# A recurrent block times a mixture of experts: four successive tokens per partition

## The chip, the core and the metric

The kernel runs on one core of a Trainium2 chip. The core has a matrix engine (TensorE, in the profile PE, with its weight loads as PEld), a vector engine (VectorE, DVE), an activation engine (ScalarE, ACT), GpSimd (POOL) and SyncE (SP), which here issues transfers only. Each engine runs its own queue in order and waits on semaphores for the others. On-chip memory is SBUF, and PSUM takes the results of matmuls; both have 128 partitions. [...]

The metric is device time in microseconds (us) from start to end of one execution. Lower is better.

## What is computed

The input `x` is (16, 512, 256) in fp32: 16 sequences, 512 tokens, 256 channels. The reference, cut to what matters:

```python
x  = L0_attn_x
xn = layernorm(x)
s  = rwkv(xn)                 # along time in each sequence
g  = silu(moe(xn))            # 8 experts; tokens are given out by top-k
return x + s * g

# rwkv(x)
x  = ln(x, ln0_w, ln0_b); h = ln(x, ln1_w, ln1_b)
xx = time_shift(h)                         # the token before
xk = h*tmk + xx*(1 - tmk)                  # and xv, xr likewise
k, v, sr = xk @ Wk.T, xv @ Wv.T, sigmoid(xr @ Wr.T)
att  = scan over t of a running weighted mean of v, weights exp(k)
x  = x + (sr*att) @ Wo.T
h2 = ln(x, ln2_w, ln2_b)
xk2, xr2 = mixes of h2 and its time shift
kv = square(relu(xk2 @ Wfk.T)) @ Wfv.T
return x + sigmoid(xr2 @ Wfr.T) * kv

# moe(x): xt is (8192, 256)
probs = softmax(xt @ Wg)
for each expert: its 1024 best tokens      # ties by token number
each token goes to its best expert among those that took it
out = weight * (gelu(xt @ W1[e]) @ W2[e])
```

Two orders matter. Time shift, the scan and the breaking of ties need a sequence's tokens in time order. A matmul that gives tokens on partitions can take them in any order, as long as everything else uses the same.

## The kernel before, in words

A sequence `b` has 512 tokens. In token-major tiles (`x`, `n`, `x0`, `y`, `s`) it is a tile of 128 partitions by `NJ` = 4 by 256 channels. `rows_of` (line 169) maps DRAM to it with `(j p) c -> p j c`: block `j` of 128 successive tokens, one token of each block on a partition. A partition thus holds tokens 128 apart, and each DMA piece is one row of 256 fp32, 1 KB. In channel-major tiles (`hp`, `mix_*`, `kT`, `vT`, `erT`, `kf`) channels lie on partitions and the 512 tokens in the free dimension.

**Start.** `logits(b)` (line 232) loads a sequence as `xa`, normalizes it to `xn`, stores that to `xn_d`, transposes it on TensorE (line 219), copies the transpose out of PSUM (line 245, on ACT or DVE) and adds the router's logits to `lg`. `route` (line 256) follows: transposes, softmax, a search bit by bit for each expert's threshold, and scans (lines 345, 408) that need time order. Its pieces are issued after projections of the recurrence (`then_route`). At the end it builds by matmul (lines 431 to 463) a table of which token each slot of an expert holds: `holds` and `goes`. `row` (partition) and `tile_no` (block) give the token's number there.

**Recurrence.** `recurrent(b)` (line 578) is a generator of 9 steps. `normed` normalizes; `shifted` (line 483) transposes the result and evicts it with weight and bias into `hp`, one column to the right, so that `hp[:, h, 0:T]` is the shifted one (line 488). `mix` makes `a*h + (1-a)*shifted` with one ACT multiplication (line 495) and one DVE instruction (line 496). `project` (line 525) multiplies by a weight, 128 output channels by 512 tokens. `wkv` (line 535) runs the scans and ends with line 567, which writes the result over `v`. `token_major` (line 569) takes 128 tokens of a channel-major tile as the stationary operand and gives token-major output; it serves `Wo`, `Wfr` and `Wfv`. The hidden layer `kf` is evicted with Relu (line 632) and squared (line 633). `L627` copies `x` to `out` from DRAM to DRAM.

**Experts.** `expert(i)` (line 655) loads `W1` and `W2` of its expert, gathers 2 x 128 rows of `xn_d` by index (line 664), and scatters its results to `ys_d` by index (line 695).

**Outputs.** For `b` below 14 `keep` (line 731) stores the recurrence's result in `s_d`; `outputs` loads it again as `s` with `y` from `ys_d`, applies Silu (line 727), multiplies (line 728) and adds to `out` by an accumulating DMA issued by POOL (line 729). The last two sequences go there directly (`put`).

The order is written by hand: `steps` (lines 759 to 764) interleaves three sequences, and `rest_of` deals out the logits of sequences 4 to 15 over steps 0 to 5, the 36 sure expert units over steps 24 to 124, the outputs from step 124 on. Buffers: `x`, `w1`, `w2` two each, `tok` three, `f4` four, three PSUM banks for projections (`mm`).

Of the kernel before, what the change touches and what calls it, by code (L numbers as in the profile page):

```python
# [9 lines left out]
F32 = mybir.dt.float32  # L10
I32 = mybir.dt.int32
BF16 = mybir.dt.bfloat16
AF = mybir.ActivationFunctionType
ALU = mybir.AluOpType
# [5 lines left out]
P = 128  # L20
# [6 lines left out]
def rwkv_times_moe_kernel(ctx: ExitStack, tc: tile.TileContext, a, out: bass.AP):  # L27
# [67 lines left out]
    nc.vector.tensor_copy(count, up)  # L95
    count_s = const.tile([P, P], BF16, name="count_s")
    nc.vector.tensor_copy(count_s, up)
# [7 lines left out]

    tiles = iota("tiles", [[1, NJ], [NJ, B]] + [[0, P // NT]])
    tile_no = const.tile([P, NT], F32, name="tile_no")
    nc.vector.tensor_copy(tile_no, tiles.rearrange("p (t r) -> p t r", r=P // NT)[:, :, 0])
    ones = const.tile([P, 1], F32, name="ones")
# [59 lines left out]
    def rows_of(t, b):  # L169
        return t[b * T : (b + 1) * T].rearrange("(j p) c -> p j c", p=P)  # L170

    x_rows, out_rows = x.rearrange("b t c -> (b t) c"), out.rearrange("b t c -> (b t) c")


# [12 lines left out]
    def load(src, b, name, tag="x", bufs=2):  # L187
        t = work.tile([P, NJ, C], F32, tag=tag, bufs=bufs, name=f"{name}{b}")
        nc.sync.dma_start(t, rows_of(src, b))
        return t  # L190
# [24 lines left out]
    def transposed(src, h, name):  # L215

        ps = pp_tr.tile([P, T], F32, tag="tr", name=f"{name}_{h}")
        for j in range(NJ):
            nc.tensor.transpose(ps[:, j * P : (j + 1) * P], src[:, j, h * P : (h + 1) * P], ident)
        return ps  # L220
# [11 lines left out]
    def logits(b):  # L232
        g = slice(b * NJ, (b + 1) * NJ)
        xt = load(x_rows, b, "xa", tag=("w1", "w2")[b % 2])
        mv, rs = mv_all[:, g, :], rs_all[:, g]
        moments(mv, xt, f"a{b}")
        inv_std(rs, mv[:, :, 1])
        xn = work.tile([P, NJ, C], F32, tag="kf", bufs=KF, name=f"xn{b}")
        normalize(xn, xt, mv[:, :, 0], rs, f"a{b}")
        nc.sync.dma_start(rows_of(xn_d, b), xn)  # L240
# [15 lines left out]
    def route():  # L256
# [4 lines left out]
        ]  # L261
        nc.vector.tensor_copy(buf[0], lg)
        yield
# [89 lines left out]
        for j in range(NJ):  # L353
            nc.tensor.transpose(ps2[:, j * P : (j + 1) * P], gt[:, j * P : (j + 1) * P], ident)
        nc.vector.tensor_copy(buf[2], ps2)
# [68 lines left out]
        nc.vector.tensor_single_scalar(lo_i, slot, P - 1, ALU.bitwise_and)  # L424
        lo = work.tile([P, NT], BF16, tag="lo", name="lo")
# [57 lines left out]
    def shifted(n, wname, bname, name):  # L483

        hp = in_turn(hps)
        for h in range(NC):
            ps = transposed(n, h, f"nps_{name}")
            nc.scalar.activation(hp[:, h, 1:], ps, AF.Identity, bias=col(bname, h), scale=col(wname, h))
        return hp

    def mix(hp, tm, name):

        m = f4(f"mix_{name}")
        for h in range(NC):
            nc.scalar.mul(m[:, h, :], hp[:, h, 0:T], col(tm, h, rest))
            nc.vector.scalar_tensor_tensor(  # L496
                m[:, h, :], hp[:, h, 1:], col(tm, h), m[:, h, :], ALU.mult, ALU.add
            )
        return m
# [25 lines left out]
    def project(w, src, o, name):  # L525

        ps = pp_mm.tile([P, T], F32, tag="mm", name=name)
        for h in range(NC):
            mm = nc.tensor.matmul(  # L529
                ps, lhsT=w[:, h, o * P : (o + 1) * P], rhs=src[:, h, :], start=(h == 0), stop=(h == NC - 1)  # L530
            )
        then_route(mm)
        return ps

    def wkv(kT, vT, erT, h, name):
# [30 lines left out]
        nc.vector.reciprocal(den, den)  # L566
        nc.vector.tensor_tensor(v, ba0[:, 1, :], den, ALU.mult)

# [9 lines left out]
    def recurrent(b, done):  # L578
# [46 lines left out]
        xk2 = mix(hp2, "cmk", f"k2{b}")  # L625
        xr2 = mix(hp2, "cmr", f"r2{b}")
        nc.sync.dma_start(rows_of(out_rows, b), rows_of(x_rows, b))  # L627
        kf = []
        for q in range(NH // 2):
            t = work.tile([P, 2, T], F32, tag="kf", bufs=KF, name=f"kf{b}_{q}")  # L630
            for o in range(2):
                nc.scalar.activation(t[:, o, :], project(wfk, xk2, q * 2 + o, f"f_{b}_{q}_{o}"), AF.Relu)  # L632
            nc.scalar.activation(t, t, AF.Square)  # L633
            kf.append(t)
# [89 lines left out]
    def output(b, s, y):  # L724
        for j in range(NJ):
            t = j * B + b
            nc.scalar.activation(y[:, j, :], y[:, j, :], AF.Silu, scale=weight_of[:, t : t + 1])  # L727
        nc.vector.tensor_tensor(s, s, y, ALU.mult)
# [101 lines left out]
```

## Time and profile before

| | |
|---|---|
| median of 3 runs | 1306.62 us (1304.05 to 1310.38) |
| the profiled execution | 1304.01 us, its span 1302.2 us |
| mean granted TensorE clock | 0.941 |
| weight loads for TensorE | 778.3 us, 60% of the span |
| ACT, DVE busy | 733.3 us (56%), 762.6 us (59%) |
| DMA from SP's queue | 88,044 packets, 97.02 MB, 23.3% of 16 engines' span |
| DMA from POOL's queue | 15,360 packets, 27.27 MB, 9.4% |
| out store (line 729), issue to landing | 5.8 to 8.5 us |

The profile is one execution recorded by the hardware. An engine's busy time is the sum over its instructions. A group of instructions is shown as line, engine, operation, what it writes and reads, shapes and count; after the bar come busy time in all, the mean of one in ns, and how long the engine was idle just before them with what ended the wait. In a timeline a row is start, duration, engine, line, operation, and in brackets the idle time before it. Span rows by stage give each engine's busy time with the number of its instructions, then the clock granted to TensorE, the mean busy share of the 16 DMA engines and GB/s. The forty slices show the busy share in tenths.

### The profile page before, as it was taken

Reading aid. Unit: us, or ns where it says so; the run is one execution under the profiler, and the core shown is the slowest. Engines: PE = TensorE matmul, PEld = TensorE weight load, DVE = VectorE, ACT = ScalarE, POOL = GpSimd, SP = SyncE. Lnnn points to the kernel's source line nnn. Section 1 sums busy time; section 2 is a strip of 40 time slices with the busy share of each in tenths; the row PEclk is TensorE's granted clock in tenths of the full one; section 3 lists DMA queues with packets and bytes.
Section 4 is the critical chain, followed back from the end, with each engine's and each line's share of the span. In section 5 each row is a group of like instructions: output and inputs, shape, how many; then the busy total and the mean of one; then the engine's idle time right before and its main releaser. Section 6 shows DMA issues by size and latency. Waiting matters only on the chain. (4 is left out here: it accounts for less than half of the span.)

```text
span 1302.2 us, 12606 instructions
## 1 busy us (share of the span) xinstructions
PE 1141.6 (88%) x4333; PEld 778.3 (60%) x4333; DVE 762.6 (59%) x1248; ACT 733.3 (56%) x1187; POOL 333.3 (26%) x427
## 2 busy tenths in 40 slices
PE   5687979569989999899989999898999989795966
PEld 2344645335848667585856768585766857463635
DVE  4699675995481745647273565717456363566651
ACT  3685766137373655738275572728448283684951
POOL 3442030042312324132151423214231230213020
PEclk7799999788989999999999999999999999898978
DMA  6895010211303313131221423122322310278391
GB/s 200 289 297 151 1 33 1 81 41 33 109 12 114 101 61 130 49 125 52 85 94 50 129 79 97 51 84 94 95 83 68 110 66 17 98 158 206 84 191 24
DMA packets 103469, 125.11 MB, mean 96 GB/s; under 512 B 5847, under 2 KB 89325, under 8 KB 103405
## 3 DMA queue, kind: packets, MB, share of 16 engines
q1 hardware_dynamic: 88044, 97.02, 23.3%
q0 software_dynamic: 15360, 27.27, 9.4%
q8 instruction: 35, 0.57, 0.2%
q14 instruction: 30, 0.24, 0.1%
HBM read 90.72 MB, written 41.94 MB: 102 GB/s over the span
## 5 line engine op out<-in xcount | busy, mean ns | idle before, releaser
L529 PE MATMUL f<-mix_k,WfkT_sb 128*128 128x512 f32 x512 | 241.0, 627 | 28.2 <-DVE mix_k L496 23.2
L572 PE MATMUL kv<-WfvT_sb,kf 128*128 128x256 f32 x1024 | 228.9, 380 | 0.0
L695 POOL DMA_INDIRECT ys_d<-ys,goes x72 | 75.9, 1054 | 528.5 <-ACT ys L693 333.4
L572 PEld LDWEIGHTS kv<-WfvT_sb,kf 128*128 128x128 f32 x1024 | 193.6, 190 | 25.9
L529 PEld LDWEIGHTS f<-mix_k,WfkT_sb 128*128 128x128 f32 x512 | 100.0, 201 | 153.1 <-issue 105.2
L646 DVE SCALAR_TENSOR_TENSOR frs<-frs,kv 128x512 f32<-128x512 f32 x32 | 21.9, 683 | 249.0 <-PE kv L572 249.0
L572 PE MATMUL y<-w,act 128*128 128x256 f32 x576 | 132.1, 379 | 0.2 <-ACT act L686 0.2
L681 PE MATMUL h<-xsT,w 128*128 128x256 f32 x576 | 130.2, 379 | 0.0
L572 PEld LDWEIGHTS y<-w,act 128*128 128x128 f32 x576 | 107.7, 190 | 19.9 <-issue 5.9
L681 PEld LDWEIGHTS h<-xsT,w 128*128 128x128 f32 x576 | 109.4, 190 | 16.2 <-issue 1.4
L211 ACT ACTIVATE n<-x,nm,rs 128x256 f32<-128x256 f32 x128 | 68.3, 593 | 80.5 <-POOL nm L209 80.5
L664 POOL DMA_INDIRECT xs<-xn_d,holds x72 | 80.1, 1112 | 112.4 <-DVE of L462 72.3
L566 DVE RECIPROCAL ex<-ex 128x512 f32<-128x512 f32 x32 | 107.2, 3350 | 0.7
L632 ACT ACTIVATE kf<-f 128x512 f32<-128x512 f32 x128 | 74.7, 594 | 54.8 <-PE f L529 53.9
L642 ACT ACTIVATE frs<-fr 128x512 f32<-128x512 f32 x32 | 19.0, 594 | 114.8 <-PE fr L572 114.7
L572 PE MATMUL o<-WoT_sb,vT 128*128 128x256 f32 x256 | 63.9, 397 | 16.9 <-DVE frs L646 10.7
L558 DVE TENSOR_TENSOR_SCAN ba<-ex 128x512 f32<-128x512 f32 x32 | 38.8, 1213 | 66.4 <-ACT ex L557 66.3
L529 PE MATMUL v<-mix_v,WvT_sb 128*128 128x512 f32 x128 | 67.4, 666 | 11.2 <-ACT kT L601 9.3
L529 PE MATMUL r<-mix_r,WrT_sb 128*128 128x512 f32 x128 | 65.3, 655 | 13.5 <-ACT kT L601 13.5
L548 DVE TENSOR_TENSOR_SCAN pp<-wcol,kT 128x512 f32<-128x512 f32 x32 | 38.9, 1217 | 50.7 <-ACT kT L601 50.7
L693 ACT COPY ys<-y 128x512 f32<-128x512 f32 x26 | 15.2, 584 | 94.0 <-PE y L572 85.3
L633 ACT ACTIVATE kf<-kf 128x1024 f32<-128x1024 f32 x64 | 67.4, 1053 | 1.2
(210 smaller groups left out, 1866.2 us busy)
## 6 DMA issues: line engine op xcount, KB each, us to landing
w<-in_W_dram SPq DMA_DIRECT2D x72, 512.0 KB
xa<-in_x_dram SPq DMA_DIRECT2D x16, 512.0 KB
xn_d<-xn SPq DMA_DIRECT2D x16, 512.0 KB
out_dram<-in_x_dram SPq DMA_DIRECT2D x16, 512.0 KB
y<-ys_d SPq DMA_DIRECT2D x16, 512.0 KB
xc<-xn_d SPq DMA_DIRECT2D x14, 512.0 KB
s_d<-x SPq DMA_DIRECT2D x14, 512.0 KB
s<-s_d SPq DMA_DIRECT2D x14, 512.0 KB
```

The lines of the kernel that those rows point to most:

```text
L211: nc.scalar.activation(dst[:, j, :], src[:, j, :], AF.Identity, bias=nm[:, j : j + 1], scale=rs[:, j : j + 1])
L529: mm = nc.tensor.matmul(ps, lhsT=w[:, h, o * P : (o + 1) * P], rhs=src[:, h, :], start=(h == 0), stop=(h == NC - 1))
L548: nc.vector.tensor_tensor_scan(pp[:, 1:], w.to_broadcast([P, T]), k, -1e38, ALU.add, ALU.max)
L558: nc.vector.tensor_tensor_scan(ba[:, 0, 1:], ex[:, 2, :], ex[:, 0, :], 0.0, ALU.mult, ALU.add)
L566: nc.vector.reciprocal(den, den)
L572: mm = nc.tensor.matmul(ps[:, jj, :], lhsT=lhsT_of(c, j), rhs=w[:, c, :], start=(c == 0), stop=(c == n - 1))
L632: nc.scalar.activation(t[:, o, :], project(wfk, xk2, q * 2 + o, f"f_{b}_{q}_{o}"), AF.Relu)
L633: nc.scalar.activation(t, t, AF.Square)
L646: nc.vector.scalar_tensor_tensor(fr, fr, 1.0, psv, ALU.add, ALU.mult)
L664: nc.gpsimd.indirect_dma_start(out=xs[:, j, :], out_offset=None, in_=xn_d[:, :], in_offset=rows_at(holds, 2 * i + j))
L681: nc.tensor.matmul(ps[:, ff, :], lhsT=w1[:, h, (f + ff) * P : (f + ff + 1) * P], rhs=xsT[:, h, :], start=(h == 0), stop=(h == NC - 1),)
L695: nc.gpsimd.indirect_dma_start(out=ys_d[:, :], out_offset=rows_at(goes, 2 * i + j), in_=y[:, j, :], in_offset=None)
```

## The change

`rows_of` now maps `(p j) c -> p (j c)`: partition `p` holds tokens `4p` to `4p+3`, 4 KB in one run in DRAM and in SBUF. This holds for `x`, `xn_d`, `s_d`, `ys_d` and `out`, in loads, stores, the copy from `x` to `out` and the accumulating stores. Transposes of such a tile give columns in tile order (block `j`, then partition), where column `j*128 + p` is token `4p + j`. Two views are added: `tiled(t)` walks a row in tile order as it lies; `timed(t)` walks a row that lies in time order so that its elements come in tile order, with a step of four elements.

What needs time order is written in time order by the instruction that was there already. The eviction of line 488 writes `hp` through `timed`; the copy of line 245 does so with `xnT`. The projections, scans and mixes for k, v, r and xk2 then work in time order as before. On the way back, three instructions return to tile order: line 567 reads its two sources through `timed` and writes `v`; line 632 reads PSUM through `timed` and writes `kf`; the mix of `xr2` reads `hp` through `timed`. The router does the same at five places. Its table takes the token number as `4p + j` plus 512 times the sequence, with float16 in place of bfloat16, since these numbers go to 511. The index tables name DRAM rows as before.

```diff
     def rows_of(t, b):
-        return t[b * T : (b + 1) * T].rearrange("(j p) c -> p j c", p=P)
+        return t[b * T : (b + 1) * T].rearrange("(p j) c -> p (j c)", p=P)
...
+    def flat(t):
+        return t.rearrange("p j c -> p (j c)")
+    def tiled(t):
+        return t.rearrange("c (j p) -> c j p", p=P)
+    def timed(t):
+        return t.rearrange("c (p j) -> c j p", p=P)
...
-        nc.sync.dma_start(t, rows_of(src, b))
+        nc.sync.dma_start(flat(t), rows_of(src, b))
...
-            nc.any.tensor_copy(xnT[:, h, :], transposed(xn, h, f"xnps{b}"))
+            nc.any.tensor_copy(timed(xnT[:, h, :]), tiled(transposed(xn, h, f"xnps{b}")))
...
-        nc.vector.tensor_copy(buf[0], lg)
+        nc.vector.tensor_copy(tiled(buf[0]), timed(lg))
...
-        nc.vector.tensor_copy(pe, ps)
+        nc.vector.tensor_copy(timed(pe), tiled(ps))
...
-        nc.vector.tensor_tensor(gt, gt, eq, ALU.add)
+        nc.vector.tensor_tensor(tiled(rank), timed(gt), timed(eq), ALU.add)
...
-        nc.vector.tensor_scalar(one, ps3, 0.0, None, ALU.is_gt, ALU.add, accum_out=n_one)
+        nc.vector.tensor_scalar(timed(one), tiled(ps3), 0.0, None, ALU.is_gt, ALU.add, accum_out=n_one)
...
-        nc.vector.scalar_tensor_tensor(at, at, base, one, ALU.add, ALU.mult)
+        at_tiled = buf[1]
+        nc.vector.scalar_tensor_tensor(tiled(at_tiled), timed(at), base, timed(one), ALU.add, ALU.mult)
...
-            in_lo = work.tile([P, G, P], BF16, tag="kf", bufs=KF, name=f"in_lo{t0}")
+            in_lo = work.tile([P, G, P], F16, tag="kf", bufs=KF, name=f"in_lo{t0}")
...
-            nc.vector.tensor_scalar(place, one, row, None, ALU.mult)
-            nc.vector.tensor_tensor(tile_, one, spread(tile_no, t0, NS), ALU.mult)
+            nc.vector.tensor_scalar(place, one, place_of[:, t0 // B : t0 // B + 1], None, ALU.mult)
+            nc.vector.tensor_tensor(
+                seq, one, count_s[:, :B, None].to_broadcast([P, B, NS]), ALU.mult
+            )
...
-            nc.scalar.activation(hp[:, h, 1:], ps, AF.Identity, bias=col(bname, h), scale=col(wname, h))
+            nc.scalar.activation(timed(hp[:, h, 1:]), tiled(ps), AF.Identity, bias=col(bname, h), scale=col(wname, h))
...
-    def mix(hp, tm, name):
+    def mix(hp, tm, name, in_tiles=False):
...
+            m_h, now, last = m[:, h, :], hp[:, h, 1:], hp[:, h, 0:T]
+            if in_tiles:
+                m_h, now, last = tiled(m_h), timed(now), timed(last)
+            nc.scalar.mul(m_h, last, col(tm, h, rest))
+            nc.vector.scalar_tensor_tensor(m_h, now, col(tm, h), m_h, ALU.mult, ALU.add)
...
-        nc.vector.tensor_tensor(v, ba0[:, 1, :], den, ALU.mult)
+        nc.vector.tensor_tensor(tiled(v), timed(ba0[:, 1, :]), timed(den), ALU.mult)
...
-        xr2 = mix(hp2, "cmr", f"r2{b}")
+        xr2 = mix(hp2, "cmr", f"r2{b}", in_tiles=True)
...
-                nc.scalar.activation(t[:, o, :], project(wfk, xk2, q * 2 + o, f"f_{b}_{q}_{o}"), AF.Relu)
+                f = project(wfk, xk2, q * 2 + o, f"f_{b}_{q}_{o}")
+                nc.scalar.activation(tiled(t[:, o, :]), timed(f), AF.Relu)
...
-        nc.gpsimd.dma_start(rows_of(out_rows, b), s, accum_op=ALU.add)
+        nc.gpsimd.dma_start(rows_of(out_rows, b), flat(s), accum_op=ALU.add)
```

More of the change, by code (lines that the diff above doesn't have):

```diff
@@ L11 @@
 I32 = mybir.dt.int32
-BF16 = mybir.dt.bfloat16
+F16 = mybir.dt.float16
 AF = mybir.ActivationFunctionType
@@ L95, in rwkv_times_moe_kernel @@
     nc.vector.tensor_copy(count, up)
-    count_s = const.tile([P, P], BF16, name="count_s")
+    count_s = const.tile([P, P], F16, name="count_s")
     nc.vector.tensor_copy(count_s, up)
@@ L104, in rwkv_times_moe_kernel @@
     nc.vector.tensor_scalar(lower, up, row, None, ALU.is_gt)
-    tiles = iota("tiles", [[1, NJ], [NJ, B]] + [[0, P // NT]])
-    tile_no = const.tile([P, NT], F32, name="tile_no")
-    nc.vector.tensor_copy(tile_no, tiles.rearrange("p (t r) -> p t r", r=P // NT)[:, :, 0])
+    place_i = const.tile([P, NJ], I32, name="place_i")
+    nc.gpsimd.iota(place_i, [[1, NJ]], base=0, channel_multiplier=NJ)
+    place_of = const.tile([P, NJ], F32, name="place_of")
+    nc.vector.tensor_copy(place_of, place_i)
     ones = const.tile([P, 1], F32, name="ones")
@@ L239, in logits @@
         normalize(xn, xt, mv[:, :, 0], rs, f"a{b}")
-        nc.sync.dma_start(rows_of(xn_d, b), xn)
+        nc.sync.dma_start(rows_of(xn_d, b), flat(xn))
         if b < AT_HAND:
@@ L353, in route @@
         for j in range(NJ):
-            nc.tensor.transpose(ps2[:, j * P : (j + 1) * P], gt[:, j * P : (j + 1) * P], ident)
+            nc.tensor.transpose(ps2[:, j * P : (j + 1) * P], rank[:, j * P : (j + 1) * P], ident)
         nc.vector.tensor_copy(buf[2], ps2)
@@ L412, in route @@
         for j in range(NJ):
-            nc.tensor.transpose(ps4[:, j * P : (j + 1) * P], at[:, j * P : (j + 1) * P], ident)
+            nc.tensor.transpose(ps4[:, j * P : (j + 1) * P], at_tiled[:, j * P : (j + 1) * P], ident)
         slot_f = work.tile([P, NT], F32, tag="red", name="slot_f")
@@ L424, in route @@
         nc.vector.tensor_single_scalar(lo_i, slot, P - 1, ALU.bitwise_and)
-        lo = work.tile([P, NT], BF16, tag="lo", name="lo")
+        lo = work.tile([P, NT], F16, tag="lo", name="lo")
         nc.vector.tensor_copy(lo, lo_i)
@@ L428, in route @@
         nc.vector.tensor_single_scalar(hi_i, slot, P.bit_length() - 1, ALU.logical_shift_right)
-        hi = work.tile([P, NT], BF16, tag="hi", name="hi")
+        hi = work.tile([P, NT], F16, tag="hi", name="hi")
         nc.vector.tensor_copy(hi, hi_i)
         table = pp_sm.tile([P, 3, NS], F32, tag="sm", name="table")
-        G = 16
+        G = B
         def spread(v, t0, n):
@@ L441, in route @@
             )
-            in_hi = work.tile([P, G, 3, NS], BF16, tag="ex", bufs=2, name=f"in_hi{t0}")
-            one, place, tile_ = (in_hi[:, :, i, :] for i in range(3))
+            in_hi = work.tile([P, G, 3, NS], F16, tag="ex", bufs=2, name=f"in_hi{t0}")
+            one, place, seq = (in_hi[:, :, i, :] for i in range(3))
             nc.vector.tensor_tensor(
@@ L457, in route @@
         nc.vector.tensor_copy(of, table)
-        nc.vector.scalar_tensor_tensor(of[:, 1, :], of[:, 2, :], float(P), of[:, 1, :], ALU.mult, ALU.add)
+        nc.vector.scalar_tensor_tensor(of[:, 1, :], of[:, 2, :], float(T), of[:, 1, :], ALU.mult, ALU.add)
         nc.vector.tensor_copy(holds, of[:, 1, :])
@@ L487, in shifted @@
             ps = transposed(n, h, f"nps_{name}")
-            nc.scalar.activation(hp[:, h, 1:], ps, AF.Identity, bias=col(bname, h), scale=col(wname, h))
+            nc.scalar.activation(timed(hp[:, h, 1:]), tiled(ps), AF.Identity, bias=col(bname, h), scale=col(wname, h))
         return hp
-    def mix(hp, tm, name):
+    def mix(hp, tm, name, in_tiles=False):
         m = f4(f"mix_{name}")
         for h in range(NC):
[L495 to L498, printed above, removed]
+            m_h, now, last = m[:, h, :], hp[:, h, 1:], hp[:, h, 0:T]
[3 more added lines that the diff above has]
+            nc.vector.scalar_tensor_tensor(m_h, now, col(tm, h), m_h, ALU.mult, ALU.add)
         return m
@@ L728, in output @@
         nc.vector.tensor_tensor(s, s, y, ALU.mult)
-        nc.gpsimd.dma_start(rows_of(out_rows, b), s, accum_op=ALU.add)
+        nc.gpsimd.dma_start(rows_of(out_rows, b), flat(s), accum_op=ALU.add)
     def keep(b, x0):
-        nc.sync.dma_start(rows_of(s_d, b), x0)
+        nc.sync.dma_start(rows_of(s_d, b), flat(x0))
     def put(b, x0):
```

## The prediction

> **What bounds the kernel.** I read the engine totals first, then the forty slices, then busy times stage by stage, then the groups with what ended the idle time before them, and last the order of time where TensorE stands still.
>
> ```profile
> PE 1141.6 (88%) x4333; PEld 778.3 (60%) x4333; DVE 762.6 (59%) x1248; ACT 733.3 (56%) x1187; POOL 333.3 (26%) x427
> ...
> DMA  6895010211303313131221423122322310278391
> ...
> DMA packets 103469, 125.11 MB, mean 96 GB/s; under 512 B 5847, under 2 KB 89325, under 8 KB 103405
> ...
> 0.00:132.00 132.00, 90.67 (x293) 45.32 (x294) 97.46 (x278) 79.43 (x146) 51.59 (x111) 0.87 0.73 231
> 132.00:297.00 165.00, 125.73 (x486) 80.44 (x485) 126.15 (x231) 84.76 (x155) 26.91 (x26) 0.87 0.10 31
> 297.00:1122.00 825.00, 790.93 (x3120) 567.98 (x3120) 446.54 (x634) 454.76 (x699) 222.86 (x259) 0.98 0.25 80
> 1122.00:1256.00 134.00, 100.25 (x324) 62.35 (x324) 83.87 (x96) 98.98 (x163) 28.09 (x28) 0.88 0.65 150
> 1256.00:1302.00 46.00, 33.97 (x112) 22.21 (x112) 8.64 (x11) 15.39 (x28) 3.85 (x4) 0.83 0.43 68
> ```
>
> The columns of the stage rows are length, busy time of PE, weight loads, DVE, ACT, POOL, then clock, DMA share and GB/s. From 297 to 1122 us TensorE is busy 791 of 825 us and the DMA engines a quarter: faster transfers buy nothing there. DMA is heavy in two places only, the first 132 us and the last 180, where TensorE idles 41 and 46 us. So the change can win only at the two ends, and what it costs on ACT and DVE it pays everywhere.
>
> **The gain: 4 KB runs.** The 122 half-megabyte transfers of x, xn_d, s_d, y and out (64 of the 125 MB) change their runs from 1 KB to 4 KB; weights and rows gathered by index stay as they are.
>
> ```profile
> 17.00:19.00 2.00, 1.07 (x6) 0.60 (x6) 0.00 (x0) 1.83 (x4) 1.75 (x5) 1.00 1.04 418
> 34.00:40.00 6.00, 0.00 (x0) 0.00 (x0) 3.98 (x19) 0.36 (x1) 1.98 (x6) 0.50 1.09 384
> ```
>
> The second row is a saturated stretch of loads in 1 KB runs, 384 GB/s; the first is mostly WfkT, whose rows are 4 KB, 418. So a load gains some 9%. [...]
>
> *Start.* DVE waits for xa 9.7 us in five places: 3.16 for the first load, 2.94 at 36 us, then 1.19, 1.64 and 0.78. The load behind the 2.94 stands behind a 1 MB weight that is not changed. From 66 to 132 us DVE itself is busy 62.4 of 66 us, so it takes over where DMA recedes. Between 0 and 4 us; I take 2.
>
> *Tail.* Accumulating stores hold DMA: 203 GB/s at a share of 1.05 from 1166 to 1174, about half the loads' rate. No row shows a 4 KB accumulate; it lies between no faster and twice as fast. What it can buy is read here:
>
> ```profile
> 1170.60 1.23 DVE L563 SCALAR_TENSOR_TENSOR ba<-ba,ex 128x1024 f32<-128x1024 f32 x1
> 1175.93 1.23 DVE L728 TENSOR_TENSOR s<-s,y 128x1024 f32<-128x1024 f32 x1 [4.11 <-ACT hp L488]
> ...
> 1178.38 1.22 DVE L728 TENSOR_TENSOR s<-s,y 128x1024 f32<-128x1024 f32 x1 [0.62 <-ACT mix_v L495]
> 1179.52 3.34 DVE L566 RECIPROCAL ex<-ex 128x512 f32<-128x512 f32 x1
> ```
>
> DVE runs in order, and the recurrence (L565, L566, L567) is queued behind two output products. The chain of waits shows what holds them: an out store of 10.63 us, then s<-s_d of 3.72, landing at 1178.26. TensorE idles 8.6 us until vT is ready. Halving the store would bring the second product forward 3 to 5 us; then y's Silu is late next. For the tail 0 to 8, taken 4.
>
> *End.* The last store is bare: POOL issues from 1293.3 in 1.28 us, bytes flow until about 1298.6, and the span ends at 1302.2. An index scatter of 128 rows takes POOL 1.00 us, so 128 runs in place of 512 save 0.3; the flow of 3.6 us may shrink by a third, 1.2. Together 1.5 (0 to 3). The sixteen out<-x copies are hidden beside compute: nothing. SP's issues (0.36 to 0.46 us each) are off the path: nothing.
>
> Gain in all 7.5, between 0 and 15.
>
> **The cost: a step of four elements, 16 bytes.** No instruction is added on the main path, but these now step through one operand or more:
>
> ```profile
> L488 ACT ACTIVATE hp<-nps,cols 128x512 f32<-128x512 f32 x64 | 47.7, 780 | 35.7 <-PE nps L219 35.5
> ...
> L632 ACT ACTIVATE kf<-f 128x512 f32<-128x512 f32 x128 | 74.7, 594 | 54.8 <-PE f L529 53.9
> L567 DVE TENSOR_TENSOR vT<-ba,ex 128x512 f32<-128x512 f32 x32 | 21.9, 684 | 0.7
> L529 PE MATMUL f<-mix_k,WfkT_sb 128*128 128x512 f32 x512 | 241.0, 627 | 28.2 <-DVE mix_k L496 23.2 <-ACT kf L632 3.1 <-ACT act L686 1.7
> ```
>
> Besides: L245 (18 on ACT, 14 on DVE), the half of mix_r that feeds xr2 (32 on each engine, L495 and L496), and five router operations (L262, L282, L347, L380, L409). TensorE's own operands stay contiguous, so its 1141.6 us stay.
>
> Does a step cost? The nearest row is L108, which reads every second int32: 64 elements in 180 ns, against 194 for the plain cast at L417. By it a step is free, but it is of 8 bytes. [...] From below the cost is nothing; I rule out a gain, since no operation gets shorter. From above I estimate half rate: a contiguous DVE operation of 1024 elements takes 1.22 us and of 512 0.68, so 512 elements are 0.54 us; on ACT 1.053 (L633) less 0.594 gives 0.46. [...]
>
> What of it ends on the path:
>
> - **hp to mix to f.** Both L488 halves precede the first mix_k on ACT, and TensorE waited for mix_k before f 11 times (23.2 us). 11 x 2 x 0.46 = 10. Behind L488 on ACT stand the mixes and the kf evictions.
> - **Start, 36 to 104 us.** DVE-bound: 13 L245 on DVE and one L567; about half of 14 x 0.54 reaches TensorE, 4; TensorE's own queue covers the rest.
> - **Router end, 223 to 241 us.** TensorE starves while DVE works through the route: L347 and L409, 2 x 0.54 = 1.
> - **Tail.** ACT is busy 99 of 134 us; 8 L488 and 7 L495 of mix_r there, about half of these for xr2: 12 x 0.46 = 5.5, of which a half, 3.
> - **The steady stage otherwise.** mix_r (x32) and L567 (x32) sit on a DVE that is busy 447 of 825 us; vT's delay reached TensorE twice (5.2 us), so 1.
>
> Sum 19, between 0 and, with PSUM doubled too, 27: an f pair takes TensorE 3.4 us and ACT 2 x 0.6 + 1.05 = 2.25; with 2 x 0.46 more it is 3.2, and beside the recurrence's exponentials ACT is just full, some 0.5 us for each of 16 batches.
>
> Float16 for bfloat16 is the same width: L439, L445, L449 keep 2.29, 1.45, 1.45 us. The smaller iota is hidden at the start. L347 and L409 write elsewhere at equal count.
>
> **Sum.** 1304.0 (the profiled execution: span 1302.2 and 1.8 around it) - 7.5 + 19 = 1315.5. The median of the runs is 2.6 higher, so 1318.
>
> **Rivals.**
>
> 1. *Steps are free, the ends win.* 1304.0 - 7.5 + 2.6 = 1299, between 1291 and 1306. For it: L108, and a store chain that plainly holds TensorE. [...] It decides if L488 stays near 780 ns and the out store lands in half its 8.5 us.
> 2. *PSUM reads double too.* 1304.0 - 7.5 + 27 + 2.6 = 1326, to 1336 if the gains fail and ACT stalls f more. For it: L632 is the largest group touched, 128 times. Against: ACT idles 53.9 us for f just before these.
> 3. *Nothing to see.* The accumulate still moves in small pieces, and steps cost a fraction: gain 3, cost 3, about 1307. For it: TensorE's 88%, and the covers named above.
>
> **How the numbers follow.** Forecast (SBUF steps at half rate) 0.42; rival 1, 0.33; rival 2, 0.13; rival 3, 0.12. A measurement of this kernel tells about 0.5%, 6.5 us, from no change. The forecast gives slower 0.36, same 0.05, faster 0.01; rival 1 faster 0.27, same 0.06; rival 2 slower 0.13; rival 3 same 0.09, faster 0.02, slower 0.01. Faster 0.30, same 0.20, slower 0.50. The forecast's own range is 1308 to 1328; with rival 1 and most of rival 2, 1290 to 1334.
>
> **What would show it.** L488's mean (1.2 us by the forecast, 0.78 by rival 1), L567's (1.2 or 0.68), L632's (0.59, or 1.05 by rival 2); the wait of f for mix_k grown by about 10 us; out stores landing in under 6 us; packets near 57,000 (64 MB in 4 KB pieces instead of 1 KB: 47,000 fewer) in place of 103,469. I am wrong in mechanism if the steps cost nothing, or if the ends win more than 10 us, which would mean that DMA held more of the start than DVE's five waits show.

## The result, and the profile after

| | before | after |
|---|---|---|
| median | 1306.62 us | 1338.66 us (1337.62 to 1340.04, 4 runs) |
| ratio | | 1.0249, 95% interval 1.0221 to 1.0276 |
| profiled span | 1302.2 us | 1335.5 us |
| TensorE clock, mean | 0.941 | 0.939 |

The change costs 32 us. The direction was forecast. The size was not: 1318 us is 11 us over before, a third of what was measured, and 1338.7 lies above the forecast's own range of 1308 to 1328.

First the engine totals, the DMA slices and the packet count of the kernel after.

```profile
PE 1155.3 (87%) x4333; PEld 782.7 (59%) x4333; DVE 795.9 (60%) x1248; ACT 780.5 (58%) x1187; POOL 323.0 (24%) x427
...
DMA  7643010302203313131131313113221320268281
...
DMA packets 54828, 125.11 MB, mean 94 GB/s; under 512 B 5846, under 2 KB 26860, under 8 KB 54508
```

Nearly half the packets are gone. ACT works 47 us more, DVE 33, and TensorE, whose instructions are the same, 14 (e1 below, without a step and no slower than before, has 5 of these 14 too: 1146.4 us). The stage rows show where the span grew (columns as before; the cuts follow the work to its later times).

```profile
0.00:132.00 132.00, 91.81 (x274) 44.41 (x275) 93.99 (x256) 81.00 (x131) 46.35 (x107) 0.83 0.55 195
132.00:306.00 174.00, 131.89 (x504) 84.35 (x502) 142.50 (x252) 97.51 (x170) 23.41 (x28) 0.88 0.14 49
306.00:1151.00 845.00, 793.97 (x3118) 567.88 (x3119) 462.37 (x635) 481.56 (x700) 227.84 (x261) 0.98 0.25 80
1151.00:1290.00 139.00, 104.33 (x327) 63.99 (x325) 86.93 (x97) 103.39 (x162) 22.80 (x29) 0.87 0.59 146
1290.00:1335.00 45.00, 33.26 (x112) 22.04 (x112) 10.09 (x11) 17.03 (x28) 2.58 (x3) 0.88 0.33 63
```

The steady stage, 825 us before, takes 845; the start up to it 9 more; the last two stages 5 and -1. In the first row the DMA share falls from 0.73 to 0.55, and TensorE's first f batch (the 32 matmuls of one sequence's hidden layer) still starts later, at 141.8 us for 130.4: the end of the start did not follow the DMA share. The groups with stepped operands, by shape (busy, mean ns, idle before them):

```profile
L547 PE MATMUL f<-mix_k,WfkT_sb 128*128 128x512 f32 x512 | 249.1, 643 | 37.0 <-DVE mix_k L516 25.2 <-ACT act L705 6.8 <-ACT kf L651 4.8
...
L505 ACT ACTIVATE hp<-nps,cols 128x512 f32<-128x512 f32 x64 | 76.8, 1267 | 39.0 <-PE nps L233 39.0
...
L651 ACT ACTIVATE kf<-f 128x512 f32<-128x512 f32 x128 | 74.2, 592 | 44.0 <-PE f L547 43.2
...
L515 ACT ACTIVATE mix_r<-hp,rest 128x512 f32<-128x512 f32 x64 | 58.7, 968 | 0.0
...
L233 PE MATMUL nps<-ident,n 128*128 128x128 f32 x256 | 38.2, 285 | 11.2 <-ACT n L225 9.7 <-ACT hp L505 1.4
...
L585 DVE TENSOR_TENSOR vT<-ba,ex 128x512 f32<-128x512 f32 x32 | 35.2, 1099 | 0.7
...
L296 DVE COPY route_w<-ps_pe 128x512 f32<-128x512 f32 x1 | 1.1, 1072 | 1.4 <-PE ps_pe L295 1.4
...
L276 DVE COPY route_w<-lg 128x512 f32<-128x512 f32 x1 | 0.7, 691 | 2.6 <-PE lg L261 2.6
```

And mix_r before:

```profile
L495 ACT ACTIVATE mix_r<-hp,rest 128x512 f32<-128x512 f32 x64 | 42.7, 717 | 0.0
```

A stepped SBUF write of hp takes 1267 ns where it took 780; vT, which reads with the step, 1099 for 684. Of the 64 muls of mix_r half are stepped, so the mean of 968 for 717 is +0.50 us each. The stepped PSUM read of kf costs nothing (592 for 594). L296 and L276 show both in one kernel: a DVE copy that writes SBUF with the step, 1072 (660 before); one that reads PSUM with it, 691 (692 before). The first row bears a surprise: f waits for mix_k only 2 us longer in all (25.2 for 23.2), yet its matmuls are slower (643 for 627 ns) and wait for other things too.

The tail, DVE in order of time, beside the stretch shown of before:

```profile
1200.71 1.23 DVE L581 SCALAR_TENSOR_TENSOR ba<-ba,ex 128x1024 f32<-128x1024 f32 x1
1205.44 1.23 DVE L747 TENSOR_TENSOR s<-s,y 128x1024 f32<-128x1024 f32 x1 [3.50 <-DMA s<-s_d]
1206.58 0.69 DVE L583 SCALAR_TENSOR_TENSOR ex<-erT,ba 128x512 f32<-128x512 f32 x1
1207.84 1.23 DVE L747 TENSOR_TENSOR s<-s,y 128x1024 f32<-128x1024 f32 x1 [0.57 <-DMA s<-s_d]
1208.98 3.35 DVE L584 RECIPROCAL ex<-ex 128x512 f32<-128x512 f32 x1
```

The recurrence still stands behind an output product that waits for s<-s_d. The accumulating stores ahead of it have not become short (KB each, median us from issue to landing), after:

```profile
out_dram<-s POOLq DMA_DIRECT2D x14, 512.0 KB, 8.5
```

Before, the trace recorded only one of these 14 landings, also 8.5. Two runs below, which differ in their runs alone and have all 14, settle it: first e4_steps_only with 1 KB runs, then e2_old_order with 4 KB.

```profile
out_dram<-s POOLq DMA_DIRECT2D x14, 512.0 KB, 8.2
...
out_dram<-s POOLq DMA_DIRECT2D x14, 512.0 KB, 8.4
```

With a quarter of the packets the store lands as late as before. Only its issue on POOL is shorter, 0.86 us for 1.28.

### The profile page after: what moved, and what is told of

Its sections match the earlier page's. It is cut to its first block, busy times and chain, and to the rows that moved or that the text cites. A ratio compares the mean times of both kernels' runs of the same rounds, so it can differ in the third digit from the quotient of the medians.

```text
span 1335.5 us, 12615 instructions
## 1 busy us (share of the span) xinstructions
PE 1155.3 (87%) x4333; PEld 782.7 (59%) x4333; DVE 795.9 (60%) x1248; ACT 780.5 (58%) x1187; POOL 323.0 (24%) x427
## 4 chain that ended last, share of the span: by engine, by line
PE 42%; ACT 22%; DVE 21%; POOL 6%; issue 6%; DMA 3%; POOLq 0%; another core or an unknown queue 0%; DVEq 0%; SPq 0%; ACTq 0%
PE f L547 13%; PE kv L590 12%; PE h L700 5%; PE y L590 4%; ACT hp L505 3%; PE fr L590 3%; ACT n L225 3%; ACT ex L575 2%; DVE ex L584 2%; DVE st L215 2%; POOL rs L209 2%; DVE mix_k L516 1%; ACT L575 1%; PE lg L261 1%; DVE ba L576 1%
## 5 line engine op out<-in xcount | busy, mean ns | idle before, releaser
L547 PE MATMUL f<-mix_k,WfkT_sb 128*128 128x512 f32 x512 | 249.1, 643 | 37.0 <-DVE mix_k L516 25.2
L714 POOL DMA_INDIRECT ys_d<-ys,goes x72 | 78.7, 1094 | 548.4 <-ACT ys L712 344.0
L590 PEld LDWEIGHTS kv<-WfvT_sb,kf 128*128 128x128 f32 x1024 | 193.9, 191 | 25.3
L505 ACT ACTIVATE hp<-nps,cols 128x512 f32<-128x512 f32 x64 | 76.8, 1267 | 39.0 <-PE nps L233 39.0
L590 PE MATMUL o<-WoT_sb,vT 128*128 128x256 f32 x256 | 67.0, 411 | 19.3 <-DVE frs L665 10.0
L547 PE MATMUL v<-mix_v,WvT_sb 128*128 128x512 f32 x128 | 63.1, 627 | 10.8 <-ACT kT L619 8.9
L712 ACT COPY ys<-y 128x512 f32<-128x512 f32 x26 | 15.1, 581 | 94.1 <-PE y L590 85.3
```

The costliest lines, as they stand in the source:

```text
L505: nc.scalar.activation(timed(hp[:, h, 1:]), tiled(ps), AF.Identity, bias=col(bname, h), scale=col(wname, h))
L547: mm = nc.tensor.matmul(ps, lhsT=w[:, h, o * P : (o + 1) * P], rhs=src[:, h, :], start=(h == 0), stop=(h == NC - 1))
L590: mm = nc.tensor.matmul(ps[:, jj, :], lhsT=lhsT_of(c, j), rhs=w[:, c, :], start=(c == 0), stop=(c == n - 1))
L714: nc.gpsimd.indirect_dma_start(out=ys_d[:, :], out_offset=rows_at(goes, 2 * i + j), in_=y[:, j, :], in_offset=None)
```

## The experiments

Comparing the instruction queues of the two kernels brought up a third suspect beside the steps and the runs: the instructions stand in another order, although no line was moved. One line decides it. The copy from `x` to `out` (L645) used to be 128 x 4 pieces of 1 KB; flattened, it is 16 pieces of 32 KB, and with it the framework's scheduler lays all five queues out differently. Steps, and the other runs, leave the order as it is: in the traces TensorE's 4333 instructions stand in one sequence in before, e2, e4, e16 and e17 and in another in after, e1 and e3. So steps, runs and order can be set apart. In the table "runs" means those of all plain transfers but this copy, which goes with the order. Each ratio is to the kernel before, run again on the same chip; its medians there were 1305.5 to 1308.3 us.

| run | order | runs | steps | median us | ratio to before, 95% |
|---|---|---|---|---|---|
| e3_order_only | new | 1 KB | none | 1310.41 | 1.0044 (1.0027 to 1.0062) |
| e1_no_steps | new | 4 KB | none | 1303.53 | 0.9979 (0.9968 to 0.9990) |
| e16_runs_old_order | old | 4 KB | none | 1300.43 | 0.9957 (0.9943 to 0.9971) |
| e4_steps_only | old | 1 KB | all | 1340.61 | 1.0280 (1.0256 to 1.0305) |
| e2_old_order | old | 4 KB | all | 1338.25 | 1.0255 (1.0235 to 1.0276) |

**e1_no_steps**

```diff
     def timed(t):
-        return t.rearrange("c (p j) -> c j p", p=P)
+        return t.rearrange("c (j p) -> c j p", p=P)
```

> The changed kernel with every stepped operand made contiguous (the tokens then stand in the order of the tiles where the recurrence expects time order, so that part of the computation is left out). It keeps the 4 KB runs and the changed order of the queues. Theory S (the steps' own durations carry the loss, 64 hp writes at +0.49 us and the rest): the time falls back to before or a little under it, 1299 to 1308 us. Theory O (the new order of the instructions carries it): it stays at 1330 to 1339. Theory M (order costs the start's 8 to 10 us, steps the rest): 1312 to 1318.

1303.5 us: theory S. The steps carry all of the loss, 35 us in this order.

**e2_old_order**

```diff
-        nc.sync.dma_start(rows_of(out_rows, b), rows_of(x_rows, b))
+        nc.sync.dma_start(*(t[b * T : (b + 1) * T].rearrange("(j p) c -> p j c", p=P) for t in (out_rows, x_rows)))
```

> The changed kernel with one line put back: the copy of x to out moves runs of 1 KB as before. The order of the instructions on every engine is then that of the kernel before, with the steps and the other 4 KB runs kept. Theory S: 1334 to 1340 us, as the changed kernel. Theory O: 1304 to 1310. Theory M: 1328 to 1331.

1338.3 for 1338.7: with the steps in it the order makes no difference that can be seen.

**e3_order_only** (an edit of the kernel before)

```diff
-        nc.sync.dma_start(rows_of(out_rows, b), rows_of(x_rows, b))
+        nc.sync.dma_start(*(t[b * T : (b + 1) * T].rearrange("(p j) c -> p (j c)", p=P) for t in (out_rows, x_rows)))
```

> The kernel before with one line of the change: the copy of x to out moves runs of 4 KB and more. No step, all other DMAs in 1 KB runs, but the instructions in the changed kernel's order. Theory S: 1304 to 1310 us. Theory O: 1330 to 1339. Theory M: 1314 to 1317.

1310.4, between S and M. Without steps the order costs 3.5 to 8 us by its interval, and e1 over e16 says 3. In the profiled execution TensorE's first f batch starts 6.9 us later than before, the third 0.9, and the span is the same (1302.0 for 1302.2). But that execution, of 1303.8 us, is the fastest of the seven; the others took 1309.6 to 1311.7. So I can't say where the few us of the timed runs lie.

**e4_steps_only**

```diff
-        return t[b * T : (b + 1) * T].rearrange("(p j) c -> p (j c)", p=P)
+        return t[b * T : (b + 1) * T].rearrange("(j p) c -> p j c", p=P)
...
     def flat(t):
-        return t.rearrange("p j c -> p (j c)")
+        return t
...
-    nc.gpsimd.iota(place_i, [[1, NJ]], base=0, channel_multiplier=NJ)
+    nc.gpsimd.iota(place_i, [[P, NJ]], base=0, channel_multiplier=1)
```

> The changed kernel with all DMAs in runs of 1 KB as before, so in the order of the kernel before, but with all stepped operands (they then put the tokens in another order than time, so that the recurrence's order is left out). Theory S: 1334 to 1342 us, and 0 to 8 above the run with the old order and the 4 KB runs if these bring anything. Theory O: 1304 to 1312. Theory M: 1328 to 1338.

1340.6: the steps alone, without a single longer run, cost what the change costs.

### Which steps

**e5_hp_plain**

```diff
-            nc.scalar.activation(timed(hp[:, h, 1:]), tiled(ps), AF.Identity, bias=col(bname, h), scale=col(wname, h))
+            nc.scalar.activation(hp[:, h, 1:], ps, AF.Identity, bias=col(bname, h), scale=col(wname, h))
```

> The changed kernel with the 64 writes of hp alone contiguous (time order is left out of both recurrent branches); all other steps, runs and the order stay. Theory F (the forecast's terms: only the waits of f for mix_k that exist before grow): 10 us in the steady stage and 3 in the tail come back, 1324 to 1328 us. Theory H (all four hp writes of a sequence lie on the path of 16 sequences, 16 x 4 x 0.49 = 31 us): 1307 to 1312. If the loss lies in the other steps: 1335 to 1339.

1321.9, ratio 1.0145 (1.0115 to 1.0175): 16.7 us come back, a little more than theory F and half of theory H.

**e6_xnT_plain**

```diff
-            nc.any.tensor_copy(timed(xnT[:, h, :]), tiled(transposed(xn, h, f"xnps{b}")))
+            nc.any.tensor_copy(xnT[:, h, :], transposed(xn, h, f"xnps{b}"))
```

> The changed kernel with the 32 evictions of xnT alone contiguous (the logits then stand in another order of the tokens than the routing takes them for). Theory F: 4 us come back, 1333 to 1336 us. Theory H leaves the start its whole lag, 8 to 10 us: 1328 to 1331. If the later stages swallow the start's lag: 1337 to 1339.

1331.5, ratio 1.0211 (1.0188 to 1.0235): 7.2 us, between the two theories.

**e7_v_xr2_plain**

```diff
-        nc.vector.tensor_tensor(tiled(v), timed(ba0[:, 1, :]), timed(den), ALU.mult)
+        nc.vector.tensor_tensor(v, ba0[:, 1, :], den, ALU.mult)
...
-        xr2 = mix(hp2, "cmr", f"r2{b}", in_tiles=True)
+        xr2 = mix(hp2, "cmr", f"r2{b}")
```

> The changed kernel with the two ways back into tiles contiguous: the 32 writes of v on DVE and the 32 plus 32 of mix_r on ACT and DVE (the second branch's tokens then stand in another order than x0's). Theory F: 1 us, 1336 to 1339 us. Theory H: 0 to 4 us, 1334 to 1339. A rival V (v is what o waits for, 16 x 2 x 0.415 = 13 us, and mix_r delays kf's evictions): 1322 to 1328.

1327.6, ratio 1.0181 (1.0158 to 1.0204): 11.1 us, rival V, and neither theory of mine. **e9_v_plain** undoes only the first of these two edits.

> The changed kernel with the 32 writes of v on DVE alone contiguous (the tokens enter x0 in another order than they stand there). It parts the 11 us that v and mix_r together gave back. Theory X (mix_r carries it: two muls on ACT, +0.5 us each, stand ahead of kf's evictions, so that f's banks come free later): 1335 to 1338 us. Theory V (v carries it, since o waits for it): 1327 to 1331.

1338.1, ratio 1.0239 (1.0217 to 1.0262): v gives back nothing, mix_r all. In sum 16.7 + 7.2 + 11.1 = 35.0, what e1 gave back at once. The sizes are less sure than this sum looks: by ratios to the runs of before of the same chip the three are 14, 5 and 9, 28 of e1's 35, each with an interval of some 3 us either way; the profiled spans say 17.7, 7.1 and 11.7. All three counts put them in the same order, and that they add up is not shown. The starts of TensorE's f batches, in us later than in e1, which has the same order and no step, show where each group works:

| batch | after | hp plain (e5) | xnT plain (e6) | v, mix_r plain (e7) | e8 |
|---|---|---|---|---|---|
| 1 | 8.1 | 4.0 | 1.3 | 7.9 | 1.1 |
| 5 | 10.0 | 4.1 | 3.2 | 6.8 | 1.2 |
| 9 | 17.9 | 8.2 | 11.2 | 13.5 | 5.2 |
| 13 | 27.8 | 11.5 | 21.0 | 17.1 | 8.5 |
| 16 | 33.5 | 15.1 | 26.7 | 21.0 | 11.7 |

xnT's 7 us are all there at the first batch and stay. Those of hp and mix_r gather over the sixteen sequences.

Why mix_r? Here is the ninth f batch, order of time, ACT and PE, after:

```profile
771.78 2.36 ACT L505 ACTIVATE hp<-nps,cols 128x512 f32<-128x512 f32 x2
...
775.09 2.36 ACT L515 ACTIVATE mix_r<-hp,rest 128x512 f32<-128x512 f32 x2
...
776.70 1.88 PE L547 MATMUL f<-mix_k,WfkT_sb 128*128 128x512 f32 x4
...
780.07 1.28 ACT L705 ACT_TABLE_LOAD   x1
...
781.36 1.08 ACT L705 ACTIVATE act<-h 128x512 f32<-128x512 f32 x2
...
782.01 13.98 PE L547 MATMUL f<-mix_k,WfkT_sb 128*128 128x512 f32 x28 [3.43 <-ACT act L705]
```

And the same in e7:

```profile
767.39 2.35 ACT L505 ACTIVATE hp<-nps,cols 128x512 f32<-128x512 f32 x2
...
770.68 1.34 ACT L515 ACTIVATE mix_r<-hp,rest 128x512 f32<-128x512 f32 x2
...
775.95 1.08 ACT L705 ACTIVATE act<-h 128x512 f32<-128x512 f32 x2
...
776.60 12.28 PE L547 MATMUL f<-mix_k,WfkT_sb 128*128 128x512 f32 x28 [2.41 <-ACT act L705]
```

f's first four matmuls start as soon as mix_k is there. The fifth needs a PSUM bank: h of the experts shares the three banks with f, and ACT's gelu (L705) has yet to empty one; from hp to that gelu ACT runs without a gap: 9.58 us after, 8.56 in e7, and the 1.02 between them is mix_r's 2.36 less 1.34. ACT is busy 58% of the span, but here it is full, and whatever stands in its queue ahead of the gelu is on TensorE's path. In this batch the wait then costs more than its length: the same stretches with the granted clock (the third number from the end), after and e7.

```profile
777.00:782.00 5.00, 1.58 (x4) 0.38 (x2) 5.00 (x4) 4.94 (x7) 2.09 (x2) 1.00 0.42 133
782.00:784.00 2.00, 1.99 (x4) 0.88 (x5) 2.00 (x3) 1.43 (x3) 1.46 (x2) 0.71 0.18 66
784.00:786.00 2.00, 2.00 (x4) 0.96 (x3) 1.97 (x2) 0.93 (x2) 1.84 (x1) 0.50 0.23 66
```

```profile
772.60:776.60 4.00, 1.59 (x4) 0.38 (x2) 4.00 (x4) 3.94 (x5) 1.80 (x2) 1.00 0.48 166
776.60:778.60 2.00, 2.00 (x5) 1.04 (x6) 2.00 (x4) 1.42 (x3) 1.60 (x2) 1.00 0.18 66
```

After 3.43 us of idling TensorE was granted 0.71 of its clock and then 0.50 (782 to 786 us); after 2.41 it had all of it, 1.00 (776.6 to 778.6). The other 28 matmuls of this batch take 13.98 us after and 12.28 in e7. So here 1.0 us of mix_r became 2.7. The length of the wait does not decide it, though. Two other waits in the same execution of e7, with the clock behind each:

```profile
385.12 14.00 PE L547 MATMUL f<-mix_k,WfkT_sb 128*128 128x512 f32 x32 [3.28 <-DVE mix_k L516]
...
679.28 2.90 PE L547 MATMUL v<-mix_v,WvT_sb 128*128 128x512 f32 x4 [2.54 <-ACT kT L619]
```

```profile
385.30:387.30 2.00, 2.00 (x5) 0.88 (x6) 2.00 (x4) 1.97 (x3) 0.00 (x0) 1.00 0.00 0
680.20:683.60 3.40, 3.40 (x5) 1.33 (x4) 3.37 (x9) 2.01 (x4) 1.33 (x2) 0.50 0.00 0
```

After 3.28 us of idling the clock stayed whole (1.00), after 2.54 it was halved (0.50). So the length of a wait does not tell whether a later gelu costs clock, and that it did in other batches is not shown. Nor can the share be read from the whole span: TensorE's busy time times the missing clock, summed over stretches of 2 us from 300 us on, is 25 us before, 29 after and 25 in e7, but 38 in e2, whose span is after's within 0.4 us. What the totals do say, one execution each: of the 11.7 us between the spans of after and e7, 6.0 are busy time of TensorE (1155.3 for 1149.3), that is slower matmuls, and 5.7 idle time.

**e13_mix_r_dve** parts mix_r by engine.

```diff
-            if in_tiles:
-                m_h, now, last = tiled(m_h), timed(now), timed(last)
-            nc.scalar.mul(m_h, last, col(tm, h, rest))
-            nc.vector.scalar_tensor_tensor(m_h, now, col(tm, h), m_h, ALU.mult, ALU.add)
+            part = m_h if half is None else half[:, h, :]
+            nc.scalar.mul(part, last, col(tm, h, rest))
+            if half is not None:
+                m_h, now, part = tiled(m_h), timed(now), timed(part)
+            nc.vector.scalar_tensor_tensor(m_h, now, col(tm, h), part, ALU.mult, ALU.add)
...
-        xr2 = mix(hp2, "cmr", f"r2{b}", in_tiles=True)
+        xr2 = mix(hp2, "cmr", f"r2{b}", half=kT)
```

> The changed kernel with mix_r's two muls on ACT contiguous, in time order, into kT, which is dead by then; the addition on DVE reads that and hp with the step and writes tiles. Nothing is left out. It parts the 11 us of mix_r by engine. Theory X (ACT: the muls stand ahead of the gelu's and kf's evictions in ACT's full queue): all of it comes back, 1326 to 1330 us. If DVE's share carries it: 1336 to 1340.

1331.4, ratio 1.0195 (1.0169 to 1.0221): 7.2 of the 11 us come back, just short of theory X's range. So ACT's muls carry most, not all; that DVE's addition is the rest was not tried apart. Its rows: the muls are at 711 ns again, DVE's addition is stepped.

```profile
L517 DVE SCALAR_TENSOR_TENSOR mix_r<-hp,cols,kT 128x512 f32<-128x512 f32 x32 | 35.7, 1156 | 0.0
...
L514 ACT ACTIVATE mix_r<-hp,rest 128x512 f32<-128x512 f32 x32 | 21.2, 711 | 0.0
```

### Where a step is free

**e8_pe_step** lets TensorE take the step.

```diff
-        nc.tensor.transpose(ps[:, j * P : (j + 1) * P], src[:, j, h * P : (h + 1) * P], ident)
+        nc.tensor.transpose(timed(ps)[:, j, :], src[:, j, h * P : (h + 1) * P], ident)
...
-            nc.any.tensor_copy(timed(xnT[:, h, :]), tiled(transposed(xn, h, f"xnps{b}")))
+            nc.any.tensor_copy(xnT[:, h, :], transposed(xn, h, f"xnps{b}"))
...
-            nc.scalar.activation(timed(hp[:, h, 1:]), tiled(ps), AF.Identity, bias=col(bname, h), scale=col(wname, h))
+            nc.scalar.activation(hp[:, h, 1:], ps, AF.Identity, bias=col(bname, h), scale=col(wname, h))
```

> The changed kernel with the step of hp and xnT moved to TensorE: each transpose writes every fourth column of its PSUM bank, and the evictions read and write contiguously; nothing is left out. If a stepped write into PSUM is as free as the stepped reads of PSUM were, both groups' cost is gone at once: by theory F 1318 to 1323 us, by theory H 1301 to 1310. If TensorE pays for the step (384 transposes at twice 0.146 us are 56 us more on the engine that bounds): 1350 to 1395.

1316.7, ratio 1.0101 (1.0075 to 1.0128): 22.0 us, of the 23.9 that hp and xnT gave back one by one. Its groups:

```profile
L505 ACT ACTIVATE hp<-nps,cols 128x512 f32<-128x512 f32 x64 | 47.7, 780 | 39.8 <-PE nps L233 39.8
...
L233 PE MATMUL nps<-ident,n 128*128 128x128 f32 x256 | 38.2, 286 | 10.3 <-ACT n L225 9.7 <-ACT hp L505 0.5
```

hp is at 780 ns again and the transposes take 286 ns, in the kernel after 285. For these transposes the step into PSUM costs TensorE nothing that can be seen.

**e10_pe_step_load** is e8 with v and mix_r left in time order.

```diff
-                token_major(lambda c, j: vT[:, c, j * P : (j + 1) * P], wo, NC, j0 + jj, ps, jj)
+                token_major(lambda c, j: timed(vT[:, c, :])[:, j, :], wo, NC, j0 + jj, ps, jj)
...
-                token_major(lambda c, j: xr2[:, c, j * P : (j + 1) * P], wfr, NC, j0 + jj, psr, jj)
+                token_major(lambda c, j: timed(xr2[:, c, :])[:, j, :], wfr, NC, j0 + jj, psr, jj)
```

> The stepped PSUM writes of the transposes as in the run before them, and v and mix_r left in time order: o and fr then load their weights from every fourth column of the SBUF tile. No stepped operand is left on ACT or DVE but the PSUM reads of kf and five of the routing; nothing is left out. If a weight load with a 16-byte step costs nothing on the path: 1316.7 - 11 = 1303 to 1308 us, with a weight load of fr at 190 ns as before. If it takes twice as long (512 loads, 0.19 us each more, of which a matmul of 0.38 us hides all but the first ones): 1305 to 1315; if none of it is hidden, 97 us more.

1311.9, ratio 1.0041 (1.0026 to 1.0056): in the second range. The rows of fr in e8, then here:

```profile
L590 PE MATMUL fr<-WfrT_sb,mix_r 128*128 128x256 f32 x256 | 61.2, 380 | 0.0
...
L590 PEld LDWEIGHTS fr<-WfrT_sb,mix_r 128*128 128x128 f32 x256 | 47.6, 190 | 8.1 <-issue 2.2 <-DVE ba L580 0.2
```

```profile
L590 PE MATMUL fr<-WfrT_sb,mix_r 128*128 128x256 f32 x256 | 66.8, 403 | 0.0
...
L590 PEld LDWEIGHTS fr<-WfrT_sb,mix_r 128*128 128x128 f32 x256 | 62.7, 326 | 2.2 <-issue 1.0 <-DVE ba L580 0.2
```

A stepped weight load takes 326 ns for 190. It runs beside a matmul of 380, but not quite hidden: the matmuls of fr become 403, 5.6 us busy more, those of o 424 for 418 in e8. Of the 11 us of v and mix_r, 5 came back; these slower matmuls, on the engine that bounds, fit what is missing, though no run shows them alone.

**e11_all_on_pe** adds to e10 the routing's five steps, moved to its transposes in two ways, of which this shows one each; **e12_all_on_pe_old_order** adds e2's edit to that.

```diff
-            nc.tensor.transpose(ps[:, j * P : (j + 1) * P], prob[:, j * B : (j + 1) * B, :], ident)
-        nc.vector.tensor_copy(timed(pe), tiled(ps))
+            nc.tensor.transpose(timed(ps)[:, j, :], prob[:, j * B : (j + 1) * B, :], ident)
+        nc.vector.tensor_copy(pe, ps)
...
-            nc.tensor.transpose(ps2[:, j * P : (j + 1) * P], rank[:, j * P : (j + 1) * P], ident)
+            nc.tensor.transpose(ps2[:, j * P : (j + 1) * P], timed(rank)[:, j, :], ident)
```

> As the run before, with the routing's five steps moved to its transposes too, so that no engine but TensorE has a stepped operand, PSUM reads of kf apart. 5 x 0.4 us on a chain of small steps between which TensorE does other work: 0 to 2 us less than the run before, 1301 to 1308 us.

> As the run before, with the copy of x to out in runs of 1 KB, so in the instruction order of the kernel before. If the new order costs what it cost alone (4 to 5 us): 1297 to 1304 us, and faster than the kernel before by 2 to 8. If the order made no difference here, as with the steps in it (1338.3 against 1338.7): within 2 us of the run before.

1316.3 (1.0045 to 1.0086) and 1312.7 (1.0027 to 1.0061): both miss their ranges, by 8 us and more. e11 came out 4 us above e10 where it should have been level or lower. The routing's move gained nothing, and both this and the order's 3.6 us lie within the intervals.

**e14_pe_step_mix** joins e8 and e13; **e15_pe_step_mix_old_order** adds e2's edit.

> As the run before, and hp and xnT stepped by TensorE's writes into PSUM as in the run that did this alone. ACT then has no stepped SBUF operand at all; v, mix_r's addition and the routing's five stay stepped on DVE. If the terms add (1316.7 - 11): 1304 to 1308 us. If DVE becomes the bound: 1310 to 1318.

> As the run before, in the instruction order of the kernel before (the copy of x to out in runs of 1 KB). If the order costs 4 us as it did alone: 1300 to 1304 us, which would beat both kernels; if not: 1304 to 1308.

1308.6 (1.0005 to 1.0028) and 1306.8 (0.9986 to 1.0016). With ACT free of steps on SBUF and in the old order, the change is level with the kernel before. It doesn't beat it: e16, without any step, is 6 us lower. What is left between them are the steps on DVE (v, mix_r's addition, the routing's five) and those into and out of PSUM; that the former are the 6 us was not tried apart.

### The runs

**e16_runs_old_order** joins the edits of e1 and e2.

> The changed kernel with no step at all (time order left out), in the instruction order of the kernel before: what is left is 4 KB runs in every plain DMA but the copy of x to out. It measures the forecast's gain of 7.5 us. If the gain is there: 1297 to 1301 us. If the runs bring 0 to 3 us: 1303 to 1306.

1300.4 us, 0.29 to 0.57% under before: longer runs bring 6.1 us (3.8 to 7.4).

**e17_scratch_runs** asks in which transfers. It is e16 with these, so the tokens stand as in the kernel before:

```diff
+    def tokens_of(t, b):
+        return t[b * T : (b + 1) * T].rearrange("(j p) c -> p j c", p=P)
...
-        nc.sync.dma_start(flat(t), rows_of(src, b))
+        if src is x_rows:
+            nc.sync.dma_start(t, tokens_of(src, b))
+        else:
+            nc.sync.dma_start(flat(t), rows_of(src, b))
...
-        nc.gpsimd.dma_start(rows_of(out_rows, b), flat(s), accum_op=ALU.add)
+        nc.gpsimd.dma_start(tokens_of(out_rows, b), s, accum_op=ALU.add)
```

> The tokens stand in tiles as in the kernel before, with no stepped operand and nothing left out; x and out keep their 1 KB runs and the instructions their old order. Only the kernel's own DRAM buffers (xn_d, s_d, ys_d), whose layout no one else sees, are laid out with four rows of a partition side by side and move in runs of 4 KB; the gathers' and scatters' row numbers come from the changed kernel's place_of. If the 6 us that the runs bring without steps lie in these transfers: 1299 to 1303 us, faster than both kernels. If they lie in the loads of x and the stores of out: 1304 to 1308.

1303.1 us, ratio 0.9956 (0.9940 to 0.9971): the same 0.4% as e16, faster than both kernels. So what the longer runs bring lies in `xn_d`, `s_d` and `ys_d`, where no step is needed for them; the intervals leave room for 2 to 3 us in `x` and `out` at most. Of it the profile shows 2 us at the start (first f batch at 127.7 instead of 130.4, and a lead of 2.0 stays to the last batch); the rest I couldn't place in one execution.

## Why the prediction was wrong in size

- **The step that failed:** "the steady stage otherwise", mix_r and vT at 1 us. The runs put 11 in its place (9 by ratios), none of them vT's (e7, e9). The forecast looked at DVE's slack, 447 of 825 us, and left out mix_r's muls on ACT but for the tail; e13 gives back 7 of the 11 by mending these alone. It had the right picture a few lines on, "ACT is just full", but used it only for the PSUM rival. By medians the forecast was some 20 us short: 10 by this term, 4 by hp, 3 by the start and 4 by the gain.
- *TensorE bounds, the ends are DMA's.* The first half held. But the start's end didn't follow the DMA share.
- *Gain 7.5.* 6.1 in the old order, but 3 in the new one, which the change brings. The first is near the forecast in part by luck, since its places were not. **Start, 2:** the first f batch starts 1.8 us earlier in e16. **Tail, 4 by a store of half the length:** failed. The store lands as late as before (8.4 us with 4 KB runs, 8.2 with 1 KB), and e17 has the gain without it. **End, 1.5:** the last store, from issue to landing, took 5.8 us before and 5.2 in e16; of the 0.6 the shorter issue is 0.4, and the flow did not shrink by a third. (The 5.8 to 8.5 us of the table of before are the only two landings of out stores that its trace has.) *The out<-x copies: nothing:* their form turned the order, at 3 to 5 us where no step hides it. What their longer runs do was not tried apart from that.
- *A step costs SBUF half rate, PSUM nothing.* This held: +0.49 (hp) and +0.51 (xnT, 1096 for 585) on ACT for 0.46 forecast, +0.39 to +0.42 on DVE for 0.54, and 592 for 594 ns from PSUM. No row of before shows either term: both were the author's estimates, and the one row with a step, L108 with its 8 bytes (180 ns for 194), pointed to no cost. TensorE's own stepped writes into PSUM were free too: e8's transposes took 286 ns for 285. L380 paid too and was in no term: it reads PSUM as it lies and writes SBUF with the step, and took 1070 ns for 692. Rivals 1, 2 and 3 fall with these numbers.
- *hp to mix to f, 10, and the tail, 3.* e5 gave back 16.7 (14 by ratios). That this is near is in part luck: of the wait named, f's for mix_k, 2.0 us came and not 10. The lateness shows as f's waits for act (+5.1) and kf (+1.7), to which mix_r adds, as k's wait for mix_k (+4.7), and as slower matmuls.
- *Start, 4.* e6 measured 7.2 (5 by ratios). The forecast took half of DVE's 14 instructions; whether that share was too small, or the 18 evictions on ACT that it left out count too, no run tells.
- *Router end, 1.* Not measured alone. L380 belongs to it as well, 0.4 us more; e11 found nothing to gain there.
- *TensorE's 1141.6 us stay.* They became 1155.3. Against e1, which has the same order and no step, the steps cost 34.2 us of span, of which 8.9 are TensorE's busy time and 25.3 its idle time. The instructions are the same, so the busy time is matmuls slowed, as by the half clock shown for the ninth batch; no term of the sum had that.

## What to carry to other kernels

Put a reordering where it is free: here TensorE's writes into PSUM (286 ns for 285) and the reads from it (592 for 594 on ACT, 691 for 692 on DVE) took a 16-byte step at no cost, while an instruction with a stepped SBUF operand paid (1267 for 780), and so did a weight load (326 for 190). Cost a longer instruction along its engine's queue, from where it stands to the bank or buffer that something behind it frees, not by the engine's mean slack (here ACT was busy 58% of the span, and mix_r without its steps gave back 11 us); and look at the clock granted behind a wait, which the wait's length alone did not tell here (1.00 after 3.28 us, 0.50 after 2.54). This kernel's own DRAM buffers were free to take another layout, so longer runs were had there without touching the order in which anything is computed (e17: ratio 0.9956).

## What the hardware showed unexpectedly

- On one engine an SBUF step of 16 bytes cost about the same per instruction of 128x512 fp32 here, whether it was written or read, and whether one operand had it or two: on ACT +0.49 us (hp, written) and +0.50 (mix_r, read); on DVE +0.39 (xnT, one written) and +0.42 (vT, two read).
- An accumulating store of 512 KB took 8.2 us to land with 512 runs of 1 KB (e4) and 8.4 with 128 of 4 KB (e2); only POOL's issue went from 1.28 to 0.86 us.
- Stepped weight loads took 326 ns for 190, and the matmuls beside them 403 for 380, though these last longer than the loads.
- A wait of 2.54 us was followed by half the clock (0.50) and one of 3.28 us by the whole (1.00), in one execution (e7).
- Left open: why the new order costs 3 to 5 us without the steps and nothing with them, how the steps' 35 us divide exactly among hp, xnT and mix_r, and how much of the slower matmuls is clock.
